# Two-layer graph attention on one core: transposes of float32 tiles moved from TensorE to 16-bit transposing transfers

## The chip, the cores and the metric

The kernel runs on one core of a Trainium2 chip. The time is device microseconds (us) of one execution; three executions of the kernel before took 3692.24, 3693.07 and 3693.68 us, the median is 3693.07. The engines of the core work side by side, each through its own list of instructions in order: TensorE (PE in the profile; PEld is its loading of weights), VectorE (DVE), ScalarE (ACT), GpSimd (POOL) and SyncE (SP, here the engine that starts most transfers).

## What is computed

There are 32 graphs of 512 nodes with 512 features each (`x`), and an adjacency matrix of 512x512 for each. Two attention layers follow each other, and each adds its result to `x`. Cut to what matters:

```python
h = maximum(layernorm(x), 0)
x = x + gat0(h, adj)                    # softmax over neighbours, one head of 512 features
h = maximum(layernorm(x), 0)
def gat_layer(x, mask, W, a_src, a_dst, bias, concat):
    xl = (x @ W).reshape(B, N, H, F)
    e = leaky_relu(asrc[:, :, None, :] + adst[:, None, :, :], 0.2)     # masked, then softmax over sources
    out = einsum('bsdh,bshf->bdhf', attn, xl)
    return (out.reshape(B, N, H * F) if concat else out.mean(axis=2)) + bias
g = elu(gat_layer(h, mask, W1, ..., b1, concat=True))                  # 4 heads of 256 features
x = x + gat_layer(g, mask, W2, ..., b2, concat=False)                  # 1 head of 512 features
```

Both products with weights, `h @ W1` and `g @ W2`, need their left operand with the features on the partitions, while `h` and `g` come out of the work before them with the nodes on the partitions. Between the two stands a transpose, and this is what the change moves.

## The kernel before

All values are float32; the masks are bf16. A graph's nodes are four tiles of 128 (`T = 4`). For each graph `b` the main loop emits, in this order: the masks, the product with W1 (`layer1_project`), the end of the graph before it (`load_back` of its `x` and `layer2_out`), the load of the graph after next, four times the edge weights and aggregate of a head (`layer1_scores`, `layer1_head`), then for graph `b + 1` the aggregate of layer 0 (`layer0_out`) and the input of layer 1 (`layer1_in`), for graph `b + 2` the scores of layer 0, and last the product with W2 (`layer2_project`).

That order isn't the one in which the instructions run. Each `op(...)` only records an engine or a choice of engines, a cost in nanoseconds, and what it reads and writes. The class `Plan` then makes several drafts of the whole program (a list scheduler: each engine takes the most urgent instruction that is ready by the costs), ranks the instructions anew after each by how late they may come, keeps the shortest draft and emits the instructions in its order. Once emitted, each engine's order is fixed: an instruction that waits holds up everything behind it on its engine. `on_pe`, `on_dve`, `on_act`, `on_pool` and `by_dma` give the costs. Buffers come from `slots`, a few places of each kind (three for edge weights `E`, six banks `acc` of TensorE's output, two for `x`); an instruction that opens a buffer is held back until a place is free.

The products with weights (`products`, L822) compute each 2x2 block product with seven partial products in place of eight; they need sums S1 to S4 of quarters of the left operand, which VectorE or GpSimd form (L803, L804), S1 being the sum of the two quarters of the later half of the nodes. The sums lie in places of `E`. A product of one graph is 56 matmuls for each layer. The aggregates (L627) are 64 matmuls for the four heads and 32 for each of layer 0 and layer 2.

The places that the change touches are these. In `layer1_in` four Relus (L510) write the normed tiles into a buffer of kind `h`; 16 TensorE transposes (`pe_transpose`, L487) turn them over into four banks, and ACT or DVE (`evict`, L520 and L526) copies each bank to `hT`. GpSimd then adds the bias `b2` to `x` (L750), and SP sends `x` to DRAM (L758, `spill`); it is brought back one graph later (L766). In `layer1_head` each tile's aggregate is scaled and given its bias (L893) into `v`. The bias was raised by 1 beforehand, so `v` holds z + 1, and elu(z) + 1 = max(z + 1, min(exp z, 1)) takes one Exp on ACT (L902) and one instruction on DVE (L905) for two tiles together. Eight transposes turn a head's result over, and the eviction takes the 1 off again:

```python
for k in range(nk):
    pt = Buffer("acc")
    for t in range(T):
        pe_transpose(0, pt, ..., v(t) + h1T("place"), ..., ident, t)
    evict(pt(*ROW), h1T(...), ..., N, bias=minus_one)
```

Other transposes on TensorE stay as they are: the columns spread into rows (`spread`, bank `m_bank`) and `in_lines` (L553). Transposing transfers of 16-bit values are in use already, for the masks (`transposed_mask`, L669), started by SP.

Of the kernel before, what the change touches and what calls it, by code (L numbers as in the profile page):

```python
# [10 lines left out]
BF16 = mybir.dt.bfloat16  # L11
AF = mybir.ActivationFunctionType
# [30 lines left out]
class Plan:  # L43
# [5 lines left out]
    DRAFTS = 6  # L49
# [61 lines left out]
    def latest(self, draft):  # L111
# [13 lines left out]
        for i in reversed(draft.order):  # L125
            occupied, there = self.cost(draft, i)[0], sum(self.cost(draft, i)[1:])
            for j in then[i]:
                late[i] = min(late[i], late[j] - (occupied if draft.engine[i] == "PE" == draft.engine[j] else there + self.SIGNAL))
        return late

    def draft(self, rank):
# [8 lines left out]
        lock, moving, landed = {"DVE": 0.0, "POOL": 0.0}, 0.0, []  # L140
# [23 lines left out]
        while len(draft.order) < len(ops):  # L164
# [19 lines left out]
            for buf in new:  # L184
                first = min(vacant[buf.kind], default=None)
# [24 lines left out]
            for held in moves:  # L210
                if len(landed) >= self.IN_FLIGHT:
                    at = max(at, landed[-self.IN_FLIGHT])
                moving = max(moving, at) + held
                there += moving - at
                landed.append(at + there)
# [39 lines left out]
def by_dma(n, after=2000.0):  # L255

    return 350.0, after, n / 300.0


@with_exitstack  # L260
def kernel(
# [51 lines left out]
    def places(kind, n, shape, dtype=F32, pool=big):  # L313
# [15 lines left out]
        "v": places("v", 2, [P, T, F]),  # L329
        "e": places("e", 1, [P, T // 2, F]),  # L330
        "col": places("col", 12, [P, T]),
        "ac": places("ac", 5, [P, 4, T]),
        "a_row": places("a_row", 1, [P, N]),
        "c_row": places("c_row", 1, [P, N]),
# [11 lines left out]
    plan = Plan(slots, ("x", "spill", "m0", "m0T", "m1", "m1T", "h", "hT", "pair", "xl2", "E", "E_one", "v", "a_row", "c_row", "a_bank"))  # L346
# [9 lines left out]
    minus_one = const.tile([P, 1], F32, name="minus_one")  # L356
    nc.vector.memset(minus_one, -1.0)
# [16 lines left out]
    b2_r = const.tile([P, D], F32, name="b2_r")  # L374
# [13 lines left out]
    def load_constants():  # L388
# [18 lines left out]
        fetch(HF, lambda: b1_r, rows(b1, HF), W["b1"](1), -LATER)  # L407
        fetch(D, lambda: b2_r, rows(b2, D), W["b2"](0), -LATER)
# [4 lines left out]
        for i in range(2):  # L413
# [5 lines left out]

        op(  # L420
            "DVE", on_dve(HF), lambda: nc.vector.tensor_scalar(b1_r, b1_r, 1.0, None, op0=ALU.add), W["b1"](1), W["b1"](0),
            -LATER,
        )
# [83 lines left out]
    def relu_normed(h, X, t, rstd, nmr):  # L507
# [3 lines left out]
                h.at[:, t, :D], X.at[:, t, :], AF.Relu, bias=nmr.at[:, t : t + 1], scale=rstd.at[:, t : t + 1]  # L511
            ),
            X((t, 0), (t, 1)) + rstd(0) + nmr(0), h(t),
        )

    def evict(src, dst, src_of, dst_of, n, bias=None, psum_half=False):

        def by_act():
            if bias is None:
                nc.scalar.copy(dst_of(), src_of())  # L520
            else:
                nc.scalar.activation(dst_of(), src_of(), AF.Identity, bias=bias)  # L522

        def by_dve():
            if bias is None:
                nc.vector.tensor_copy(dst_of(), src_of())  # L526
            else:
                nc.vector.tensor_scalar(dst_of(), src_of(), -1.0, None, op0=ALU.add)

        op(("ACT", "DVE"), (on_act(n, bias is not None), on_dve(n)), (by_act, by_dve), src, dst)  # L530
# [16 lines left out]
    def in_lines(ac, part, n):  # L547

        pt, flat_, lines = Buffer("acc"), Buffer("e"), Buffer("lines")
# [6 lines left out]
        evict(pt(0), flat_(0), lambda: pt.at[:m, :P], lambda: flat_.at[:m, 0, :P], P)  # L556
        op(
            "SP", by_dma(4 * m * P, 3000.0),
            lambda: nc.sync.dma_start(lines.at[:n].rearrange("n (t p) -> (n t) p", p=P), flat_.at[:m, 0, :P]),
# [4 lines left out]
    def row_of(kind, lines, k):  # L564

        row = Buffer(kind)
# [466 lines left out]
```

## Time and profile before

| what | value |
|---|---|
| median of three executions | 3693.07 us |
| the profiled execution | 3694.24 us |
| its span, first to last instruction | 3692.5 us |
| mean granted TensorE clock | 0.996 |
| one graph, once the loop is running | 112.6 us |
| busy in the span: PE, DVE, ACT, POOL | 3625.2, 2878.2, 1760.2, 1592.1 us |
| transfers: SP's queue, GpSimd's queue | 26.2%, 6.5% of 16 DMA engines' span |

Durations of single instructions come from the profiled execution. Starts of consecutive instructions on one engine lie closer than their durations say, as an instruction begins before the one ahead of it has ended; where a sum over many is wanted, the distance between starts is the measure. "Idle before, releaser" in a group's row is the time that the engine stood still just before those instructions, and what ended most of it.

### The profile page before, as it was taken

To read this page: it belongs to the slowest core of one execution; us is meant where nothing else is said; L and a number is where in the kernel's file an instruction comes from. 1 tells how busy PE (TensorE), PEld (TensorE's weight loads), DVE (VectorE), ACT (ScalarE), POOL (GpSimd) and SP (SyncE) were. 2 spreads that over 40 slices of the span, in tenths; PEclk is the share of its full clock that TensorE was granted. 3 is DMA by queue.
4 is the path that set the end of the run, shared out by engine and by line. 5 is a ranking of instruction groups with operands and counts; after the bars stand their busy time and mean duration, and the time that the engine had idled before them with its cause. 6 is when DMAs were issued, how large, how long until landed. Compare 5 with 4: busy or idle time off the path is not lost.

```text
span 3692.5 us, 51317 instructions
## 1 busy us (share of the span) xinstructions
PE 3625.2 (98%) x17806; PEld 3131.3 (85%) x17806; DVE 2878.2 (78%) x7478; ACT 1760.2 (48%) x3227; POOL 1592.1 (43%) x1353
## 2 busy tenths in 40 slices
PE   5899999999999999999999999999999999999998
PEld 4788888888888888888888888888888888888887
DVE  7988778877788877788877878777887778787755
ACT  2455444554454554445544445544455544455433
POOL 3534444534444444445344444444444444444332
PEclk9999999999999999999999999999999999999999
DMA  6244322334323333223333233442233422334310
GB/s 162 52 92 103 87 73 82 81 92 104 72 74 90 75 103 91 70 83 80 91 103 72 76 88 75 103 98 68 81 82 85 103 72 78 86 75 103 90 51 32
DMA packets 304342, 312.17 MB, mean 85 GB/s; under 512 B 150496, under 2 KB 188880, under 8 KB 304080
## 3 DMA queue, kind: packets, MB, share of 16 engines
q1 hardware_dynamic: 270288, 275.32, 26.2%
q0 software_dynamic: 33792, 33.56, 6.5%
q8 instruction: 140, 2.29, 0.3%
q14 instruction: 122, 1.00, 0.1%
HBM read 240.91 MB, written 67.89 MB: 84 GB/s over the span
## 4 chain that ended last, share of the span: by engine, by line
PE 94%; DVE 3%; DMA 1%; POOL 0%; issue 0%; ACT 0%; DVEq 0%; ACTq 0%
PE acc L627 46%; PE acc L822 41%; PE acc L487 4%; PE m_bank L487 2%; DVE junk L591 1%; DVE junk L378 0%; PE acc L553 0%; DVE E L612 0%; DMA m<-in_adj_dram 0%; DVE v L905 0%; POOL E_one L614 0%; DVE E_one L612 0%; DMA x<-in_x_dram 0%; DVE v L893 0%; DMA out_dram<-x 0%
## 5 line engine op out<-in xcount | busy, mean ns | idle before, releaser
L614 POOL TENSOR_TENSOR E<-E,m 128x512 f32<-128x512 f32 x512 | 620.2, 1240 | 803.3 <-DVE E L612 798.3
L627 PE MATMUL acc<-pair,E 128*128 128x257 f32 x4096 | 961.6, 381 | 1.4 <-ACT E L617 1.2
L627 PEld LDWEIGHTS acc<-pair,E 128*128 128x128 f32 x4096 | 743.0, 190 | 114.5 <-ACT E L617 14.4
L822 PE MATMUL acc<-w_T,E 128*128 128x257 f32 (+1 forms) x2048 | 521.5, 381 | 1.0 <-ACT pair L522 0.6
L627 PE MATMUL acc<-h,E_one 128*128 128x256 f32 (+1 forms) x2048 | 478.2, 382 | 6.3 <-ACT E_one L617 6.3
L617 ACT ACTIVATE E<-E 128x512 f32<-128x512 f32 x512 | 312.0, 624 | 315.4 <-POOL E L614 315.4
L627 PE MATMUL acc<-xl,E_one 128*128 128x257 f32 x1984 | 448.2, 379 | 0.0
L591 DVE CUSTOM_DVE_ANT_0 junk<-m1T,a_bank 128x512 bf16<-128x512 bf16 x640 | 436.0, 681 | 15.4 <-PE a_bank L487 1.7
L627 PEld LDWEIGHTS acc<-h,E_one 128*128 128x128 f32 x2048 | 383.8, 191 | 59.4 <-ACT E_one L617 7.6
L822 PEld LDWEIGHTS acc<-w_T,E 128*128 128x128 f32 x2048 | 379.6, 190 | 55.4 <-ACT pair L522 0.8
L627 PEld LDWEIGHTS acc<-xl,E_one 128*128 128x128 f32 x1984 | 371.4, 190 | 53.7
L612 DVE TENSOR_TENSOR E<-E,m_bank 128x512 f32<-128x512 f32 x512 | 326.5, 679 | 24.7 <-PE m_bank L487 24.7
L609 ACT ACTIVATE E<-c_row,ac 128x512 f32<-128x512 f32 x512 | 335.6, 708 | 1.9 <-DMA c_row<-lines 1.9
L520 ACT COPY pair<-acc 128x258 f32<-128x258 f32 (+1 forms) x375 | 138.2, 369 | 412.1 <-PE acc L822 410.3
L520 ACT COPY xl<-acc 128x257 f32<-128x257 f32 x219 | 81.7, 373 | 455.8 <-PE acc L822 455.8
L902 ACT ACTIVATE e<-v,minus_one 128x512 f32<-128x512 f32 x256 | 184.3, 720 | 236.4 <-DVE r L639 111.1
L645 DVE SCALAR_TENSOR_TENSOR x<-acc,r,x 128x256 f32<-128x256 f32 x512 | 240.6, 478 | 47.8 <-PE acc L627 43.6
L663 POOL DMA_DIRECT2D m<-in_adj_dram x64 | 51.4, 804 | 521.1 <-DVE col L591 476.8
L835 DVE TENSOR_TENSOR pair<-acc,pair 128x258 f32<-128x258 f32 (+1 forms) x390 | 164.5, 424 | 137.8 <-PE acc L822 127.7
L822 PE MATMUL acc<-w,hT 128*128 128x258 f32 x1024 | 268.4, 382 | 0.0
L822 PE MATMUL acc<-w,pair 128*128 128x257 f32 x1024 | 259.3, 380 | 0.0
L614 POOL TENSOR_TENSOR E_one<-E_one,m 128x512 f32<-128x512 f32 x128 | 145.0, 1165 | 263.2 <-DVE E_one L612 263.2
(108 smaller groups left out, 6117.7 us busy)
## 6 DMA issues: line engine op xcount, KB each, us to landing
a_row<-lines SPq DMA_DIRECT2D x190, 256.0 KB, 3.4
c_row<-lines SPq DMA_DIRECT2D x190, 256.0 KB, 3.5
x<-in_x_dram SPq DMA_DIRECT2D x32, 1024.0 KB
m<-in_adj_dram POOLq DMA_DIRECT2D x64, 512.0 KB, 7.0
spill<-x SPq DMA_DIRECT2D x32, 1024.0 KB, 4.3
x<-spill SPq DMA_DIRECT2D x32, 1024.0 KB
out_dram<-x SPq DMA_DIRECT2D x30, 1024.0 KB, 5.0
m0T<-m SPq DMA_TRANSPOSE x128, 4.2
```

Source lines behind the costliest of these rows:

```text
L487: op("PE", on_pe(P, transpose=True), lambda: nc.tensor.transpose(dst_of(), src_of(), identity), src, dst(part), ahead)
L520: nc.scalar.copy(dst_of(), src_of())
L591: lambda t=t: nc.vector.tensor_tensor_reduce(junk, mask_max.at[:, t, :], a_row.at, 1.0, LOWEST, ALU.add, ALU.max, accum_out=amax.at[:, t : ...
L609: lambda t=t: nc.scalar.activation(E.at[:, t, :], c_row.at, AF.Prelu, bias=a_of(t), scale=1.0, alpha=SLOPE),
L612: op("DVE", on_dve(N), lambda t=t: nc.vector.tensor_sub(E.at[:, t, :], E.at[:, t, :], m_row.at), m_row(*ROW) + E(t), E(t))
L614: "POOL", on_pool(N, True), lambda t=t: nc.gpsimd.tensor_add(E.at[:, t, :], E.at[:, t, :], mask.at[:, t, :]),
L617: op("ACT", on_act(N), lambda t=t: nc.scalar.activation(E.at[:, t, :], E.at[:, t, :], AF.Exp), E(t), E(t))
L627: lambda s=s: nc.tensor.matmul(acc.at[:, :n], E.at[:, s, node_block(t)], of(s), start=(s == 0), stop=(s == T - 1)),
L645: lambda acc=acc, r=r, f=f, t=t: nc.vector.scalar_tensor_tensor(X.at[:, t, f], acc.at[:, :HD], r.at, X.at[:, t, f], op0=ALU.mult, op1=ALU. ...
L822: lambda k=k: nc.tensor.matmul(acc.at[:, :width], at[a]()[:, k, node_block(r)], weight_of(w, k, c), start=(first and k == 0), stop=(k == n ...
L835: op("DVE", on_dve(width), lambda: nc.vector.tensor_add(place(), acc.at[:, :width], place()), acc(0) + token, token)
L902: op("ACT", on_act(2 * F, 1), lambda e=e, ts=ts: nc.scalar.activation(e.at, v.at[:, ts, :], AF.Exp, bias=minus_one), parts, e(0))
```

## The change

A float32 tile is turned over as two 16-bit halves. `turned` does it in three steps: ACT copies the tile of 128x512 float32, seen as 128x1024 values of 16 bits, into a second buffer so that all lower halves come first and all upper halves after them; SP starts one transposing transfer back into the first buffer, eight blocks of 128x128; ACT copies the result to its place, `hT` or `h1T`, and pairs lower and upper halves again. `layer1_in` calls it once for each node tile, `layer1_head` once for each pair of tiles of a head, so 12 times a graph.

Since such a copy can't subtract 1, the elu is now computed as max(z, -relu(1 - exp z)): Exp and a Relu on ACT, one instruction on DVE; `b1` is no longer raised. The normed tiles of layer 1 no longer take the place of kind `h`. The kinds `e`, `a_row` and `c_row`, one place each, become one kind `row` with four places, which the normed tiles, the second buffers of the turns, the elu's Exps, the rows of scores and the lines all share; `v` has four places of two tiles each, `col` and `ac` have fewer. The bias `b2` is added in DRAM: after `x` is spilled, GpSimd starts a transfer that adds `b2` to each of the 512 rows of the spilled copy. In the planner the costs of transposing transfers are new (`by_turning`, for the masks' too), transposing and other transfers are counted as two resources, and it makes 16 drafts in place of 6.

The core of the diff:

```diff
-    DRAFTS = 6
+    DRAFTS = 16
...
-                moving = max(moving, at) + held
-                there += moving - at
+                for k, held in enumerate(moves):
+                    taken[k] = max(taken[k], at) + held
+                there += max(taken[: len(moves)]) - at
...
+def by_turning(n):
+
+    return 1100.0 + n / 1000.0, 600.0, n / 300.0, 1400.0 + n / 180.0
...
-        "v": places("v", 2, [P, T, F]),
-        "e": places("e", 1, [P, T // 2, F]),
-        "col": places("col", 12, [P, T]),
-        "ac": places("ac", 5, [P, 4, T]),
-        "a_row": places("a_row", 1, [P, N]),
-        "c_row": places("c_row", 1, [P, N]),
+        "v": places("v", 4, [P, 2 * F]),
+        "row": places("row", 4, [P, N]),
+        "col": places("col", 10, [P, T]),
+        "ac": places("ac", 4, [P, 4, T]),
...
-    def relu_normed(h, X, t, rstd, nmr):
+    def relu_normed(place, token, X, t, rstd, nmr, also=()):
         op(
             "ACT", on_act(D, 2),
             lambda: nc.scalar.activation(
-                h.at[:, t, :D], X.at[:, t, :], AF.Relu, bias=nmr.at[:, t : t + 1], scale=rstd.at[:, t : t + 1]
+                place(), X.at[:, t, :], AF.Relu, bias=nmr.at[:, t : t + 1], scale=rstd.at[:, t : t + 1]
             ),
-            X((t, 0), (t, 1)) + rstd(0) + nmr(0), h(t),
-        )
-
...
+    def turned(values_of, src, e, place, results_of, dst):
+
+        def copied(out_of, in_of, reads, writes):
+            op(
+                "ACT", on_act(2 * N), lambda: nc.scalar.copy(out_of(), in_of()), reads, writes,
+            )
+
+        copied(
+            lambda: e.at.bitcast(U16).rearrange("p (b f) -> p b f", b=2),
+            lambda: values_of().bitcast(U16).rearrange("p (f b) -> p b f", b=2), src + place, e(0),
+        )
+        op(
+            "SP", by_turning(4 * P * N),
+            lambda: nc.sync.dma_start(
+                values_of().bitcast(U16).rearrange("p (c n) -> p c n", n=P), e.at.bitcast(U16), transpose=True
+            ),
+            e(0), src,
+        )
+
+        def paired():
+            out = results_of()
+            k, t = out.shape[1], out.shape[2]
+            return (
+                out.bitcast(U16).rearrange("p k t (n b) -> p k t n b", b=2),
+                values_of().bitcast(U16).rearrange("p (b t k n) -> p k t n b", b=2, k=k, t=t),
+            )
+
+        copied(lambda: paired()[0], lambda: paired()[1], src, dst)
...
-            relu_normed(hn, xb, t, rstd, nmr)
-        for k in range(KD):
-            pt = Buffer("acc")
-            for t in range(T):
-                pe_transpose(
-                    AHEAD, pt, lambda t=t, pt=pt: pt.at[:, node_block(t)], hn(t) + hT("place"),
-                    lambda t=t, k=k: hn.at[:, t, node_block(k)], ident, t,
-                )
-            evict(pt(*ROW), hT((k, 0), (k, 1)), lambda pt=pt: pt.at, lambda k=k: hT.at[:, k, :], N)
+            hn, e = Buffer("row"), Buffer("row")
+            relu_normed(lambda hn=hn: hn.at, hn(0), xb, t, rstd, nmr, e("place"))
+            turned(
+                lambda hn=hn: hn.at, hn(0), e, hT("place"),
+                lambda t=t: hT.at[:, :, node_block(t)].rearrange("p k (t n) -> p k t n", t=1), hT(*((k, t) for k in range(KD))),
+            )
...
         HT[b] = hT
-        for t in range(T):
-            op(
-                "POOL", on_pool(D), lambda t=t: nc.gpsimd.tensor_add(xb.at[:, t, :], xb.at[:, t, :], b2_r),
-                xb((t, 0), (t, 1)) + W["b2"](0), xb((t, 0), (t, 1)), lock=True,
-            )
-
 
         X.pop(b)
         S[b] = away = Buffer("spill")
         op(
             "SP", by_dma(4 * N * D), lambda: nc.sync.dma_start(away.at.rearrange("(t p) f -> p t f", p=P), xb.at),
             xb(*((t, half) for t in range(T) for half in range(2))), away(0),
+        )
+        op(
+            "POOL", (2200.0, 8000.0),
+            lambda: nc.gpsimd.dma_start(
+                away.at, bass.AP(tensor=b2.tensor, offset=b2.offset, ap=[[0, N], [1, D]]), accum_op=ALU.add
+            ),
+            away(0), away(0),
         )
 
...
-        v = Buffer("v")
-        for t in range(T):
-            acc = aggregate(E, t, xl, lambda s: ((j, s),), lambda s: xl_of(xl)[:, s, j, 2:], F + 1, v)
-            r = Buffer("r")
-            op("DVE", on_dve(8), lambda acc=acc, r=r: nc.vector.reciprocal(r.at, acc.at[:, F : F + 1]), acc(0) + xl(2), r(0))
-            op(
-                "DVE", on_dve(F, 1.0, True),
-                lambda t=t, acc=acc, r=r: nc.vector.scalar_tensor_tensor(
-                    v.at[:, t, :], acc.at[:, :F], r.at, b1_r[:, h * F : (h + 1) * F], op0=ALU.mult, op1=ALU.add
-                ),
-                acc(0) + r(0) + W["b1"](0), v(t),
-            )
-        for half in range(2):
-            ts = slice(half * T // 2, (half + 1) * T // 2)
-            parts = v(*range(T)[ts])
-            e = Buffer("e")
-            op("ACT", on_act(2 * F, 1), lambda e=e, ts=ts: nc.scalar.activation(e.at, v.at[:, ts, :], AF.Exp, bias=minus_one), parts, e(0))
-            op(
-                "DVE", on_dve(2 * F),
-                lambda e=e, ts=ts: nc.vector.scalar_tensor_tensor(
-                    v.at[:, ts, :], e.at, 1.0, v.at[:, ts, :], op0=ALU.min, op1=ALU.max
-                ),
-                parts + e(0), parts, lock=True,
-            )
         if j == 0:
             H1T.setdefault(b, []).append(Buffer("pair"))
         h1T = H1T[b][h // 2]
         nk = F // P
-        for k in range(nk):
-            pt = Buffer("acc")
-            for t in range(T):
-                pe_transpose(
-                    0, pt, lambda t=t, pt=pt: pt.at[:, node_block(t)], v(t) + h1T("place"), lambda t=t, k=k: v.at[:, t, node_block(k)], ident, t
+        for half in range(2):
+            ts = range(T)[half * T // 2 : (half + 1) * T // 2]
+            v, e = Buffer("v"), Buffer("row")
+            for i, t in enumerate(ts):
+                acc = aggregate(E, t, xl, lambda s: ((j, s),), lambda s: xl_of(xl)[:, s, j, 2:], F + 1, v)
+                r = Buffer("r")
+                op("DVE", on_dve(8), lambda acc=acc, r=r: nc.vector.reciprocal(r.at, acc.at[:, F : F + 1]), acc(0) + xl(2), r(0))
+                op(
+                    "DVE", on_dve(F, 1.0, True),
+                    lambda i=i, acc=acc, r=r, v=v: nc.vector.scalar_tensor_tensor(
+                        v.at[:, i * F : (i + 1) * F], acc.at[:, :F], r.at, b1_r[:, h * F : (h + 1) * F],
+                        op0=ALU.mult, op1=ALU.add,
+                    ),
+                    acc(0) + r(0) + W["b1"](0), v(i),
                 )
-            evict(pt(*ROW), h1T((j * nk + k, 0), (j * nk + k, 1)), lambda pt=pt: pt.at, lambda k=k: h1T_of(h1T)[:, j * nk + k, :], N, bias=minus_one)
+            op("ACT", on_act(2 * F), lambda e=e, v=v: nc.scalar.activation(e.at, v.at, AF.Exp), v(0, 1), e(0))
+            op(
+                "ACT", on_act(2 * F, 1),
+                lambda e=e: nc.scalar.activation(e.at, e.at, AF.Relu, bias=one, scale=-1.0), e(0), e(0),
+            )
+            op(
+                "DVE", on_dve(2 * F),
+                lambda e=e, v=v: nc.vector.scalar_tensor_tensor(v.at, e.at, -1.0, v.at, op0=ALU.mult, op1=ALU.max),
+                v(0, 1) + e(0), v(0, 1), lock=True,
+            )
+            turned(
+                lambda v=v: v.at, v(0, 1), Buffer("row"), h1T("place"),
+                lambda half=half: h1T_of(h1T)[:, j * nk : (j + 1) * nk, half * HN : (half + 1) * HN].rearrange(
+                    "p k (t n) -> p k t n", n=P
+                ),
+                h1T(*((j * nk + k, half) for k in range(nk))),
+            )
 
```

## The prediction

> **What bounds the kernel now.** I read the page from the top: the busy shares, then the chain that ended last, then the groups of instructions, then one period of the timeline. From the page, the busy time of each engine (busy us, share, instructions) and the chain by engine and by line:
>
> ```profile
> PE 3625.2 (98%) x17806; PEld 3131.3 (85%) x17806; DVE 2878.2 (78%) x7478; ACT 1760.2 (48%) x3227; POOL 1592.1 (43%) x1353
> ...
> PE 94%; DVE 3%; DMA 1%; POOL 0%; issue 0%; ACT 0%; DVEq 0%; ACTq 0%
> ```
>
> The reader is to see that TensorE is busy 98% and carries 94% of the chain: what leaves TensorE leaves the time, as long as nothing new makes it wait. The chain shows the same piece of layer 2's product (52 matmuls, L822) again and again at one distance:
>
> ```profile
> 1521.11 11.30 PE acc L822 x52
> 1633.73 11.30 PE acc L822 x52
> ```
>
> So one graph takes 112.6 us. Within that period (1408.5 to 1521.1 us) the engines were busy 112.60 (PE), 88.54 (DVE), 54.58 (ACT) and 49.39 us (POOL): TensorE has no gap at all. The groups to be removed, and two operations I use as prices (columns: line, engine, operation, operands, shapes, count, then busy us, mean ns, idle time before them):
>
> ```profile
> L487 PE MATMUL acc<-ident,v 128*128 128x128 f32 x1024 | 164.4, 273 | 2.4 <-DVE v L905 2.4
> L522 ACT ACTIVATE pair<-acc,minus_one 128x512 f32<-128x512 f32 x133 | 90.5, 682 | 111.8 <-PE acc L487 111.7
> L487 PE MATMUL acc<-ident,h 128*128 128x128 f32 x512 | 78.4, 278 | 7.0 <-ACT h L510 7.0
> L750 POOL TENSOR_TENSOR x<-x,b_r 128x512 f32<-128x512 f32 x128 | 162.2, 1298 | 34.6 <-ACT h L510 34.6
> ```
>
> Mean durations overlap on TensorE, so the price is the distance between starts. From the timeline of TensorE (start us, length us):
>
> ```profile
> 1476.62 0.60 PE L487 MATMUL acc<-ident,v 128*128 128x128 f32 x4
> 1477.06 2.33 PE L627 MATMUL acc<-pair,E 128*128 128x257 f32 x10
> ```
>
> Four transposes advance the engine by 0.44 us: 0.109 each. One matmul record of 128x257 advances it 0.217 us and a float32 matmul is two of them: 0.4345 us. What a 16-bit turning transfer costs, from the timeline of SP's queue and the issues (the last number is median us from issue to landing):
>
> ```profile
> 1442.73 2.51 SPq L669 DMA_TRANSPOSE m1T<-m  x2
> ...
> m0T<-m SPq DMA_TRANSPOSE x128, 4.2
> m1T<-m SPq DMA_TRANSPOSE x128, 2.4
> ```
>
> For 128x512 values of 16 bits SP is held 1.2 us; looked at in slices of 0.1 us, the data move only after that, for 0.7 us at some 215 GB/s, and it lands 0.5 us later: 2.4 in all. m0T's, which share the queues with a mask load, take 4.2.
>
> **What the Trainium skill says.** "DMA: Bandwidth & Descriptors", section "DMA Transpose (X-bar)": transposing transfers take 2-byte types only, write SBUF, and come from SP's or ACT's queue; hence the split of float32 into halves, and SP. The trace has them on SP with bf16. "VectorE: DVE Perf Modes", section "The three transpose paths", puts a 128x128 block at 390 ns on TensorE and 1309 on the transfer: TensorE's is 0.109 here when streamed, so the measurement decides; four blocks in 2.4 us fit. "SBUF — State Buffer", section "Door 1: The DMA port swizzle", says that accesses that leave a 16-byte line each time pay a penalty; the second copy alternates between halves 1 KB apart. No run here shows that pattern.
>
> **The change, part by part.** The planner's order of the changed kernel has 8590 TensorE instructions instead of 10126: 1536 transposes fewer (512 of normed inputs, 1024 of heads' results), 48 a graph. 1536 x 0.109 = 167 us off TensorE. Nothing takes their place there.
>
> ACT: 384 turns with two copies of 128x1024 16-bit values each. Price: the skill's "ScalarE: Activation LUTs", section "What ACT_TABLE_LOAD costs", has 0.833 ns an element and 93 ns between back-to-back instructions, 0.95 us (estimate); the trace's float32 Exp advances 0.53 us for 512, which agrees. 768 x 0.95 = 730 us; 256 new Relus of 0.62 (the pace of four L609 in 2.55 us) 159; evictions removed: 133 x 0.6 + 70 x 0.5 = -115. ACT goes from 1760 to about 2530 us, 71% of 3570. The first copy is safe; the second I take at 0.95 too, at most 1.9 if each access pays.
>
> DVE loses 123 + 58 evictions of 0.69 (-125 us). POOL loses L750, -162 us, for 32 accumulating transfers. Those wait on POOL for the spill to land (4.3 us), and mostly a memset and the next sums stand behind them; the sum is needed a whole graph later, when x comes back. POOL is idle over half the period, so I cost this at nothing, and 1 to 3 us a graph if its 1 MB of additions slows the turns beside it; that is not shown before.
>
> SP: 12 turns a graph of 256 KB. The issue lies between 1.36 us (the planner's figure) and 2.4 (twice 1.2); data 1.25 us at the measured rate; 0.5 to land: 3.2 to 4.2, I take 3.7 from issue to landing. SP's sum is 12 x 2 + 8 x 1.2 + about 25 x 0.4 = 44 of 107 us. Data for all: 384 x 256 KB at 215 GB/s, 470 us of a 3570 us span.
>
> What matters is whether two chains are covered. **Heads' end:** after the last aggregate, reciprocal and L893 0.64, Exp, Relu and maximum 0.7 + 0.7 + 0.7, copy 1.0, hand-overs 0.5: 4.2; turn 3.7; copy 1.0; first sum of layer 2 (POOL, L804) 1.3: 10.2 us. In the new order TensorE has 28 matmuls there (18 of layer 0's, 10 of layer 2's), 12.2 us. Covered by 2 us. The final copy stands on ACT behind two h activations that wait for layer 0's last matmuls, no later than that. **Layer 1's input:** norm 3.5, two Relus and a copy to 5.9, turn to 9.6, copy back, Relu and copy of tile 2 to 12.2 (four row buffers allow two tiles at once), turn to 15.9, then tile 3's Relu, copy back and copy to 18.5; on SP its turn is behind x coming back and two row loads, 1.5 MB at about 300 GB/s, so it lands near 23.7; copy 1.0, two sums 2.3: 27. With the accumulate beside it, 28. TensorE's cover is all 56 matmuls of layer 2's product and 16 of layer 1's: 31.5 us. Covered by 3 to 4.
>
> In between, ACT's second copies wait in order. In the new order the work on ACT between the two copies of a head's turn is 3.75 us on average by these prices, about the turn; the shorter gaps miss 1.5 us (turn 3.4) to 5.8 (turn 4.4) a graph, and ACT in the heads' stretch has 35.7 us of work against 46.1 of TensorE's. So waits are mostly absorbed; queued behind them are Exps of E and evictions of acc, for which TensorE waits if late. I allow 1 us a period, 31 in all (0 to 3 a period). The start: the first graph has nothing to lay over layer 1's input chain (TensorE waits there already), +10; the last graph's heads' end has a half of layer 2's aggregates over it and a chain 4 us longer than now, +5.
>
> Sum: span 3692.5 - 167 + 31 + 10 + 5 = 3571.5. The profiled execution took 3694.24, 1.7 more than its span and 1.2 more than the median of 3693.07; so 3572 as a median.
>
> **Rivals.** (1) Everything hides: 3525 + 15 and no stalls, 3540; DVE (44.2 busy of 46.5 us in the heads' stretch now, 2.6 of it removed) speaks a little against it. (2) The second copy runs at half rate: 8 x 0.95 = 7.6 us more in the heads' stretch, 43.3 of 46.1, and with waits of 2 to 5 us TensorE stalls some 3 us a graph more: 3571 + 31 x 3, about 3660. (3) Slower, by one mechanism: the turns take longer than planned, and ACT's in-order waits on them replace the transposes. If load costs them what it costs m0T (4.2 - 2.4 = 1.8), a turn is 5.5: the input chain becomes 28 + 3 x 1.8 = 33.4, 1.9 late; heads wait 8 x (5.6 - 3.75) = 14.8 on ACT with 10.4 spare, 4.4 late; 6.3 lost against 5.2 gained: 3693 + 31 x 1.1 + 15, about 3742. It decides from a turn of about 5.3 us on. For it: m0T's 4.2, and that order and buffers leave little to spare. Against it: in the heads' stretch the transfers are idle now (21% busy). (4) That the change doesn't do what it says is excluded by the counts.
>
> **Chances.** The likeliest case with rival 1: 0.46, its own range 3530 to 3640. Rival 2: 0.11. Within 0.2% (7 us, about what can be told from no change): 0.04. Rival 3 and worse: 0.39, of which 0.14 lies over 3850. Faster 0.57, same 0.04, slower 0.39. For 8 in 10 the range goes from 3530, where nothing stalls, to 3850.
>
> **What would show it.** Right: TensorE's transposes gone, period 107 to 109 us, ACT's copies near 1.0 us, turns landing in 3.2 to 4.2, TensorE's idle before L822 and L627 matmuls small. Wrong: ACT's longest waits on the turning transfers and TensorE idle behind late Exps or evictions; copies near 2 us; or the period ending on the sums of layer 1 whose last tile comes late. The forecast fails if turns land after 5 us or the two covers are shorter than counted.

## The result, and the profile after

The changed kernel takes 3986.54 us (median of four executions, 3979.25 to 3990.85), the kernel before beside it 3692.65: a ratio of 1.079, 95% interval 1.0775 to 1.0812. The forecast was 3572 us, with a range of 3530 to 3850. The transposes did go, and yet one graph takes 120.1 us in place of 112.6 (from start to start of the spills, five graphs on from 549.73 us; later graphs take somewhat longer: from there on it is 121.5 on average over 26 graphs).

From the page after: busy time by engine, the chain by engine and by line, then groups (columns as before) and issues of transfers.

```profile
PE 3571.2 (90%) x16270; PEld 3024.4 (76%) x16270; DVE 2775.1 (70%) x7356; ACT 2532.6 (63%) x4039; POOL 1385.6 (35%) x1206
...
PE 25%; DVE 24%; DMA 22%; ACT 20%; issue 4%; POOL 3%; SPq 1%; DVEq 0%; ACTq 0%; POOLq 0%
DMA row<-row 16%; PE acc L842 14%; PE acc L649 11%; DVE junk L613 6%; ACT row L529 4%; DVE E L634 3%; ACT row L928 3%; ACT pair L529 2%; ACT E L639 2%; DMA m<-in_adj_dram 2%; DVE x L667 2%; ACT row L925 2%; DMA row<-lines 2%; ACT hT L529 2%; ACT row L509 2%
...
L529 ACT COPY hT<-row 128x1024 uint16<-128x1024 uint16 x128 | 147.7, 1154 | 470.7 <-DMA row<-row 470.7
...
L842 PE MATMUL acc<-w_T,pair 128*128 128x257 f32 x512 | 165.4, 475 | 193.2 <-ACT xl L519 160.1
...
L529 ACT COPY pair<-v 128x1024 uint16<-128x1024 uint16 x256 | 295.1, 1153 | 20.9 <-DMA v<-row 17.8
...
L529 ACT COPY row<-v 128x1024 uint16<-128x1024 uint16 x256 | 263.3, 1038 | 28.9 <-DVE v L932 28.3
...
spill<-in_L_gnn_b_dram POOLq DMA_DIRECT2D x32, 1024.0 KB, 14.8
...
v<-row SPq DMA_TRANSPOSE x256, 3.0
```

TensorE's share of the chain fell from 94% to 25%, and the largest single entry is now a transfer, `row<-row`: the turns of layer 1's input. ACT stood 470.7 us before the copies that wait for those turns, but only 20.9 before the copies of the heads' turns, though these are twice as many. The heads' turns land in 3.0 us (the median; the profile has the landing of 29 of the 256). So turning is not slow in itself; something stands beside the input's turns. The transfer that adds `b2` takes 14.8 us from issue to landing. TensorE's largest wait follows from ACT's: 160.1 us before matmuls of layer 2's product, until ACT's eviction `xl<-acc` of earlier results of that product frees a bank.

One graph shows it. From the timeline after, engine by engine (start us, length us; in brackets the idle time before and its releaser):

```profile
1885.73 1.13 POOL L776 DMA_DIRECT2D spill<-in_L_gnn_b_dram  x1
...
1889.91 11.04 SPq L538 DMA_TRANSPOSE row<-row  x2
...
1902.04 1.16 ACT L529 COPY hT<-row 128x1024 uint16<-128x1024 uint16 x1 [10.94 <-DMA row<-row]
...
1903.26 0.36 ACT L519 COPY xl<-acc 128x257 f32<-128x257 f32 x1
...
1899.25 1.90 PE L842 MATMUL acc<-w_T,pair 128*128 128x257 f32 x8
1905.43 2.09 PE L842 MATMUL acc<-w,hT 128*128 128x258 f32 x4 [4.28 <-ACT hT L529]
...
1921.83 5.44 PE L842 MATMUL acc<-w_T,E 128*128 128x258 f32 x16 [4.14 <-POOL E L824]
```

GpSimd starts the adding transfer 4 us before the first turns. SP, whose issue of a turn otherwise takes 1.23 us (the median of the heads' turns), is held for 11 us by two of them. ACT waits 10.94 us for the first; queued behind that copy is the eviction `xl<-acc`, and TensorE, which needs the bank or the turned tile, stops for 4.28 us. Later the sums of layer 1 come late too, and it stops for 4.14. What the transfer engines carried between 1890 and 1895 us (queue, packets, MB, share of the 16 engines; q0 is GpSimd's queue, q1 is SP's):

```profile
q0 software_dynamic: 297, 0.60, 104.4%
q1 hardware_dynamic: 48, 0.01, 1.1%
```

The two turns are issued, but hardly a packet of theirs moves while the additions fill the engines; in the next 5 us GpSimd's queue takes 26.9% and SP's 109.8%. The stretches around it (length; busy us and instructions of PE, PEld, DVE, ACT, POOL; granted clock, share of the transfer engines, GB/s):

```profile
1895.00:1900.00 5.00, 5.00 (x25) 4.36 (x24) 0.85 (x2) 0.00 (x0) 0.00 (x0) 1.00 1.38 56
1900.00:1905.00 5.00, 1.15 (x6) 0.66 (x4) 0.43 (x1) 2.96 (x5) 0.00 (x0) 1.00 0.49 80
1905.00:1910.00 5.00, 4.57 (x14) 3.77 (x15) 0.13 (x1) 1.70 (x3) 0.00 (x0) 0.66 0.69 157
```

Between 1895 and 1900 the transfer engines are full (a share above 1 is packets lying over each other) and move only 56 GB/s. And after the idle time the granted clock is 0.66: part of the stall is paid a second time.

### The profile page after: what moved, and what is told of

It reads as the page before. It is cut to its first block, busy times and chain, and to the rows that moved or that the text cites. A ratio compares the mean times of both kernels' runs of the same rounds, so it can differ in the third digit from the quotient of the medians.

```text
span 3989.1 us, 49533 instructions
## 1 busy us (share of the span) xinstructions
PE 3571.2 (90%) x16270; PEld 3024.4 (76%) x16270; DVE 2775.1 (70%) x7356; ACT 2532.6 (63%) x4039; POOL 1385.6 (35%) x1206
## 4 chain that ended last, share of the span: by engine, by line
PE 25%; DVE 24%; DMA 22%; ACT 20%; issue 4%; POOL 3%; SPq 1%; DVEq 0%; ACTq 0%; POOLq 0%
DMA row<-row 16%; PE acc L842 14%; PE acc L649 11%; DVE junk L613 6%; ACT row L529 4%; DVE E L634 3%; ACT row L928 3%; ACT pair L529 2%; ACT E L639 2%; DMA m<-in_adj_dram 2%; DVE x L667 2%; ACT row L925 2%; DMA row<-lines 2%; ACT hT L529 2%; ACT row L509 2%
## 5 line engine op out<-in xcount | busy, mean ns | idle before, releaser
L649 PE MATMUL acc<-pair,E 128*128 128x257 f32 x4096 | 943.3, 382 | 25.2 <-ACT E L639 24.6
L649 PEld LDWEIGHTS acc<-pair,E 128*128 128x128 f32 x4096 | 763.1, 190 | 157.4 <-ACT E L639 51.5
L613 DVE CUSTOM_DVE_ANT_0 junk<-m1T,a_bank 128x512 bf16<-128x512 bf16 x640 | 436.4, 682 | 37.1 <-DMA row<-lines 12.1
L529 ACT COPY hT<-row 128x1024 uint16<-128x1024 uint16 x128 | 147.7, 1154 | 470.7 <-DMA row<-row 470.7
L649 PEld LDWEIGHTS acc<-h,E_one 128*128 128x128 f32 x2048 | 387.6, 190 | 69.5 <-ACT E_one L639 11.4
L519 ACT COPY pair<-acc 128x258 f32<-128x258 f32 (+1 forms) x445 | 164.7, 371 | 327.0 <-PE acc L842 325.1
L631 ACT ACTIVATE E<-row,ac 128x512 f32<-128x512 f32 x512 | 338.1, 708 | 6.0 <-DMA row<-lines 5.1
L842 PE MATMUL acc<-w_T,pair 128*128 128x257 f32 x512 | 165.4, 475 | 193.2 <-ACT xl L519 160.1
L529 ACT COPY pair<-v 128x1024 uint16<-128x1024 uint16 x256 | 295.1, 1153 | 20.9 <-DMA v<-row 17.8
L842 PEld LDWEIGHTS acc<-w_T,pair 128*128 128x128 f32 x512 | 119.2, 239 | 225.3 <-ACT xl L519 167.8
L529 ACT COPY row<-v 128x1024 uint16<-128x1024 uint16 x256 | 263.3, 1038 | 28.9 <-DVE v L932 28.3
L842 PEld LDWEIGHTS acc<-w,hT 128*128 128x128 f32 x1024 | 203.8, 203 | 86.8 <-ACT hT L529 35.8
## 6 DMA issues: line engine op xcount, KB each, us to landing
spill<-in_L_gnn_b_dram POOLq DMA_DIRECT2D x32, 1024.0 KB, 14.8
```

What stands on the lines that cost most here:

```text
L519: (lambda: nc.scalar.copy(dst_of(), src_of()), lambda: nc.vector.tensor_copy(dst_of(), src_of())), src, dst,
L529: "ACT", on_act(2 * N), lambda: nc.scalar.copy(out_of(), in_of()), reads, writes,
L613: lambda t=t: nc.vector.tensor_tensor_reduce(junk, mask_max.at[:, t, :], a_row.at, 1.0, LOWEST, ALU.add, ALU.max, accum_out=amax.at[:, t : ...
L631: lambda t=t: nc.scalar.activation(E.at[:, t, :], c_row.at, AF.Prelu, bias=a_of(t), scale=1.0, alpha=SLOPE),
L649: lambda s=s: nc.tensor.matmul(acc.at[:, :n], E.at[:, s, node_block(t)], of(s), start=(s == 0), stop=(s == T - 1)),
L842: lambda k=k: nc.tensor.matmul(acc.at[:, :width], at[a]()[:, k, node_block(r)], weight_of(w, k, c), start=(first and k == 0), stop=(k == n ...
```

## The experiments

### What the adding transfer costs

**Without it.** The planner still counts it, so the order on every engine stays; only the instruction is left out.

```diff
-            lambda: nc.gpsimd.dma_start(
-                away.at, bass.AP(tensor=b2.tensor, offset=b2.offset, ap=[[0, N], [1, D]]), accum_op=ALU.add
-            ),
+            lambda: None,
```

> The changed kernel without the adding transfer; the planner still counts it, so every engine keeps its order. b2 is left out of the result. Theory A (the adding transfer, 14.8 us from issue to landing, holds SP's queue and the turns of layer 1's input behind it): most of the 470.7 us that ACT waits for those turns goes, 3560 to 3660 us. Rival B (the chain of layer 1's input is too long even with free queues, since the turns follow each other over four row buffers): still over 3850. Rival C (ACT's in-order second copies and their 1.15 us in place of 0.95 cost the heads' stretch): over 3750, with TensorE idle behind the heads.

Measured: 3653.12 us (3649.33 to 3656.34), ratio 0.989 [0.9879, 0.9908]. The transfer costs 3986.5 - 3653.1 = 333 us, 10.4 a graph. Of the two profiled spans' difference, 334.6 us, TensorE's idle time makes 266 (417.9 against 151.8); the other 68.5 is busy time (3571.2 against 3502.7) for the same instructions in the same order, at a mean clock of 0.961 against 0.991.

**A plain copy in its place.** The same 1 MB by the same queue, read from the one row of `b2`, written elsewhere in DRAM.

```diff
-                away.at, bass.AP(tensor=b2.tensor, offset=b2.offset, ap=[[0, N], [1, D]]), accum_op=ALU.add
+                spare, bass.AP(tensor=b2.tensor, offset=b2.offset, ap=[[0, N], [1, D]])
```

> In the place of the adding transfer a plain one of the same size, from the same queue and with the same source, into a spare DRAM buffer; b2 is left out of the result. Theory A in the form that it is the adding (reading and writing back) that takes 14.8 us: the plain one lands in 5 to 8 us and the time is within 60 us of the run without any. In the form that any megabyte on GpSimd's queue holds the turns: 3850 to 3990, as with the adding.

Measured: 3890.94 us, within the range expected if any megabyte on GpSimd's queue holds the turns, though it lands sooner than the adding one. 238 of the 333 us are there without any adding.

**Another source.** `b2` is written into 512 rows of DRAM once, and the adding transfer reads those.

```diff
+    wide = spill.tile([N, D + 16], F32, tag="wide", name="wide")
+    nc.gpsimd.dma_start(wide[:, :D], bass.AP(tensor=b2.tensor, offset=b2.offset, ap=[[0, N], [1, D]]))
...
-                away.at, bass.AP(tensor=b2.tensor, offset=b2.offset, ap=[[0, N], [1, D]]), accum_op=ALU.add
+                away.at, wide[:, :D], accum_op=ALU.add
```

> The changed kernel, with b2 written once into 512 rows of DRAM and the adding transfer reading those instead of the one row again and again. If reading one row 512 times makes the transfer slow, it falls from 14.8 us to some 5 (a plain spill of 1 MB is 4.5) and most of the 333 us come back, to 3660 to 3720. If the adding in DRAM itself is slow, it stays at 13 to 15 us and the time above 3900.

Measured: 3844.68 us, between the two expectations. Then the same source and no adding:

```diff
-                away.at, wide[:, :D], accum_op=ALU.add
+                spare, wide[:, :D]
```

> As the kernel whose adding transfer reads 512 written-out rows (3845 us), but the transfer only copies those rows to another place in DRAM and adds nothing; b2 is left out. If both the repeated row and the adding cost, it lands in some 5 us instead of 10.0 and the time is 3690 to 3740. If moving 1 MB from DRAM to DRAM on this queue costs 10 us whatever it does, it stays near 10 and the time near 3840.

Measured: 3750.24 us, 10 above the range expected if both the repeated row and the adding cost. The issues of the transfer on the three pages (median us from issue to landing last), the plain copy of one row first:

```profile
spare<-in_L_gnn_b_dram POOLq DMA_DIRECT2D x32, 1024.0 KB, 10.7
```

adding from 512 rows:

```profile
spill<-wide POOLq DMA_DIRECT2D x32, 1024.0 KB, 10.0
```

and the plain copy of 512 rows:

```profile
spare<-wide POOLq DMA_DIRECT2D x32, 1024.0 KB, 6.3
```

| 1 MB by GpSimd's queue | issue to landing, us | ACT's wait for input turns, us | time, us | over no transfer |
|---|---|---|---|---|
| none | - | 107.1 | 3653 | 0 |
| copy, 512 rows | 6.3 | 225.4 | 3750 | +97 |
| add, 512 rows | 10.0 | 318.4 | 3845 | +192 |
| copy, one row read 512 times | 10.7 | 383.7 | 3891 | +238 |
| add, one row read 512 times | 14.8 | 470.7 | 3987 | +333 |

The three parts add up: moving 1 MB there at all costs 97 us, reading one row again and again 141 (in both pairs: 238 - 97, 333 - 192), adding 95 (192 - 97, 333 - 238). Over the range, each microsecond of landing costs (3987 - 3750) / (14.8 - 6.3) = 28 us, 0.87 a graph. Two limits: the middle three rows are one execution each, and four executions of the changed kernel lie 11.6 us apart; and the plain copies don't have to wait for the spill to land, so "adding" includes that wait (in the changed kernel GpSimd waits 4.5 us for it in all).

**In four pieces** of 128 rows, planned and issued one by one.

```diff
-            "POOL", (2200.0, 8000.0),
...
-            away(0), away(0),
+        for t in range(T):
+            op(
+                "POOL", (1200.0, 3700.0),
...
+                    away.at[node_block(t)], bass.AP(tensor=b2.tensor, offset=b2.offset, ap=[[0, P], [1, D]]), accum_op=ALU.add
...
+                away(t), away(t),
```

> The adding transfer of the changed kernel in four pieces of 128 rows, planned and issued one by one. If a turn waits because a whole 1 MB of additions stands ahead of it on the same DMA engines, a piece takes 14.8 / 4 = 3.7 us, no turn waits longer than some 6 us unless pieces stand back to back, and a good part of the 333 us comes back: 3750 to 3880. If the pieces are issued back to back it stays at 3950 to 4000. If the fixed part of each transfer is what costs, each piece still takes 10 us or more and the time goes above 4050.

Measured: 3874.27 us (3871.12 to 3876.42), ratio 1.049 [1.0473, 1.0508]. From its timeline of GpSimd and of SP:

```profile
1945.12 3.47 POOL L777 DMA_DIRECT2D spill<-in_L_gnn_b_dram  x4
...
1947.87 18.91 SPq L538 DMA_TRANSPOSE row<-row  x3
```

The pieces were issued back to back, for which 3950 to 4000 was expected; 112 us came back nevertheless, and the time is at the upper end of the first range. ACT's wait for the input's turns fell from 470.7 to 356.2 us, yet its longest is 14.1. Each piece lands in 9.0 us (median), so the expected 3.7 is refuted too. The planner drew up another order for the pieces, so how much of the 112 us is the size of a block and how much is the order isn't settled.

**After the turns.** The planner is told that the adding transfer reads the turned tiles, so that it puts it behind the turns in its order; nothing on the chip waits for that.

```diff
-            away(0), away(0),
+            away(0) + hT(*((k, t) for k in range(KD) for t in range(T))), away(0),
```

> The changed kernel with the adding transfer held back until the four turns of layer 1's input have been copied to hT. Theory A: the turns land in 3 to 4 us again and most of the loss goes; the transfer then stands beside the masks' transposing transfers and the rows, which have more to spare: 3680 to 3760. If any transfer of that kind beside any transposing one costs as much: over 3880.

Measured: 3932.63 us (3930.05 to 3933.94), ratio 1.065 [1.0633, 1.0665]. Two graphs from its timelines of GpSimd and ACT, one with the transfer after the turns, one with it beside the last two:

```profile
1170.09 1.13 POOL L776 DMA_DIRECT2D spill<-in_L_gnn_b_dram  x1
1275.77 1.15 POOL L776 DMA_DIRECT2D spill<-in_L_gnn_b_dram  x1 [0.43 <-issue]
...
1187.56 0.59 ACT L601 COPY a_bank<-row 128x512 f32<-128x512 f32 x1 [6.46 <-DMA row<-lines]
...
1291.70 1.16 ACT L529 COPY hT<-row 128x1024 uint16<-128x1024 uint16 x1 [10.92 <-DMA row<-row]
```

With the transfer moved away from the turns, ACT waits 6.46 us for the rows of scores (over the span 200.3 us, against 68.4 in the changed kernel); where the order slips, the transfer stands beside turns again and ACT waits 10.92 us for one. The time is in the range of the second expectation, but in the loop about every second graph is of the second kind and doesn't test what was meant, and the order is a new one. So this run only says that the place tried isn't free.

**In the kernel before.** Only `b2` is moved to DRAM, with the adding transfer of the changed kernel; all transposes stay on TensorE, the planner is the old one.

```diff
-        for t in range(T):
-            op(
-                "POOL", on_pool(D), lambda t=t: nc.gpsimd.tensor_add(xb.at[:, t, :], xb.at[:, t, :], b2_r),
...
+                away.at, bass.AP(tensor=b2.tensor, offset=b2.offset, ap=[[0, N], [1, D]]), accum_op=ALU.add
```

> The kernel before with only the addition of b2 moved into DRAM; transposes stay on TensorE. Theory A: the adding transfer costs only where turns stand behind it, so 3670 to 3710 us, no difference that matters. If adding in DRAM is itself costly (queues held for x coming back and for the rows), over 3750.

Measured: 3735.33 us (3732.05 to 3737.7), ratio 1.012 [1.0101, 1.0131], between the two expectations. The same transfer, landing in 15.7 us here, costs 43 us where only the masks' turns and row loads are near it, and 333 where every input tile passes through a turn. (GpSimd's 162 us of additions are gone in both, and the 43 us hold a new draft of the order as well.)

### What the turns bring without it

**b2 by GpSimd again**, before the spill as in the kernel before, everything else as changed (`v` has three places, as the row of `b2` takes room again).

```diff
-        "v": places("v", 4, [P, 2 * F]),
+        "v": places("v", 3, [P, 2 * F]),
...
+                "POOL", on_pool(D), lambda t=t: nc.gpsimd.tensor_add(xb.at[:, t, :], xb.at[:, t, :], b2_r),
```

> The changed kernel with b2 added by GpSimd in SBUF as before, planned anew; three places of v in place of four make room for the row of b2. Theory A: 3560 to 3660 us, faster than the kernel before. Rivals B and C: over 3750.

Measured: 3739.26 us (3736.46 to 3740.8), ratio 1.0125 [1.0108, 1.0142]. It lies between the two expectations. From its waits (us in total, times, longest):

```profile
POOL x L771 <- ACT row L511: 192.0, 87, 7.0
...
PE m_bank L488 <- DVE col L622: 53.3, 52, 4.1
PE acc L842 <- DVE pair L855: 40.0, 24, 3.9
```

GpSimd's additions must follow the Relus, which now come tile by tile with the turns, so they wait 192 us in order (34.6 before), and TensorE waits more on columns and on results that VectorE adds up (30.4 and 16.9 in the run without `b2`). Taking `b2` back into SBUF costs 3739 - 3653 = 86 us against leaving it out; three places of `v` and another order are part of that. With the additions after `x` has come back instead:

```diff
-        for t in range(T):
-            op(
-                "POOL", on_pool(D), lambda t=t: nc.gpsimd.tensor_add(xb.at[:, t, :], xb.at[:, t, :], b2_r),
...
             away(0), xb(*((t, half) for t in range(T) for half in range(2))),
         )
+        for t in range(T):
+            op(
+                "POOL", on_pool(D), lambda t=t: nc.gpsimd.tensor_add(xb.at[:, t, :], xb.at[:, t, :], b2_r),
```

> Both turned by transfers, b2 added by GpSimd in SBUF after x comes back from DRAM instead of before it leaves; three places of v. If the 86 us between the run with b2 on GpSimd and the run without any b2 come from GpSimd's additions waiting behind the late Relus of layer 1's input (192 us of waits there): 3640 to 3670 us. If they come from three places of v: still 3710 to 3750.

Measured: 3689.88 us (3683.18 to 3693.69), ratio 0.999 [0.9984, 0.9997], within 0.2% of the kernel before. It lies between the two expectations: 49 of the 86 us came back. GpSimd waits longer here than before, 339.1 us for `x` to come back, so the length of its wait alone doesn't set the price, and how the other 37 us divide between the places of `v`, the additions and the order isn't separated.

**The planner alone** in the kernel before:

```diff
-    DRAFTS = 6
+    DRAFTS = 16
...
-                "SP", (2200.0, 3000.0, 600.0),
+                "SP", by_turning(2 * P * N),
```

> The kernel before with only the planner of the changed one (16 drafts, new costs for the masks' transfers, two resources). If the planner by itself matters, over 3710 or under 3675 us; I expect 3685 to 3700, and with that the rest of the difference belongs to the turns and the addition of b2.

Measured: 3716.25 us (3714.66 to 3716.99), ratio 1.006 [1.0048, 1.0078]: 24 us lost, more than expected, so the planner matters by itself.

**Only the heads turned**: layer 1's input goes through TensorE, GpSimd adds `b2` before the spill, `v` has three places, the planner is the new one.

```diff
-            hn, e = Buffer("row"), Buffer("row")
-            relu_normed(lambda hn=hn: hn.at, hn(0), xb, t, rstd, nmr, e("place"))
-            turned(
...
+                pe_transpose(
+                    AHEAD, pt, lambda t=t, pt=pt: pt.at[:, node_block(t)], hn(t) + hT("place"),
```

> Only the heads' results turned by transfers; layer 1's input by TensorE and b2 by GpSimd in SBUF as before; three places of v. Theory D (the heads' turns are covered, as each landed in 3.0 us; what is left of the loss without the adding transfer comes from layer 1's input): 3693 - 1024 x 0.109 + 15, 3580 to 3620 us. Rival C (ACT's in-order copies cost the heads' stretch): 3660 or more.

Measured: 3654.40 us (3653.99 to 3654.76), ratio 0.990 [0.9881, 0.9911], between the two expectations. Of the kernels that leave no part out it is the fastest: 1.0% faster than the kernel before, 8.3% than the changed one. And with the planner of before (the heads' turns, which it didn't know, are priced in its form: 1240 ns of issue, 2400 ns after it, and 300 bytes a ns):

```diff
-    DRAFTS = 16
+    DRAFTS = 6
...
-                "SP", by_turning(2 * P * N),
+                "SP", (2200.0, 3000.0, 600.0),
```

> Only the heads' results are turned by transfers, layer 1's input stays with TensorE and b2 with GpSimd, as in the kernel with the heads alone (3654 us), but with the planner of before: its 6 drafts, its old costs of transfers, one resource for all of them. The planner alone cost 24 us when put into the kernel before. If that loss adds up, this comes to 3654 - 24 = 3630 (3615 to 3640). If the new costs of turning are needed for the order around the turns, it comes to 3654 or above.

Measured: 3710.37 us (3708.38 to 3713.18), ratio 1.005 [1.0033, 1.0066]. The expected 3630 is refuted: with turns in the program the new planner saves 56 us, without them it costs 24. Its price can't be taken from one kernel to the other.

**Only the input turned**, the heads on TensorE:

```diff
-        for k in range(KD):
-            pt = Buffer("acc")
...
+            turned(
+                lambda hn=hn: hn.at, hn(0), e, hT("place"),
```

> The new planner, the heads turned by TensorE as before, and only layer 1's input by transfers, four turns a graph; b2 is left out of the sum, with nothing in its place. 512 transposes fewer are 512 x 0.109 = 56 us. If the chain of the input is covered as predicted: 3716 - 56 = 3660 (3650 to 3672). If it isn't, and this is where the rest of the gain went: 3690 or above.

Measured: 3795.49 us (3789.9 to 3802.45), ratio 1.028 [1.0265, 1.0296]: 79 us above the planner alone, where 56 below was forecast. From its chain (start us, length us), one graph:

```profile
1583.20 5.12 DMA row<-row
...
1592.56 11.58 PE acc L849 x52
...
1606.18 1.19 SPq L705
1607.41 1.26 SPq L705
1608.72 1.26 SPq L705
...
1611.60 8.03 DMA row<-lines
```

In this graph the product with `hT` runs on without a gap; what ends late are the rows of scores. Their loads stand on SP behind the issues of the masks' turns, and then take 8 us (7.2 in the median; 3.7 and 3.4 for the two rows under the planner alone). Over the whole span the loads of rows and the input's turns have 6% of the chain each, so one graph doesn't settle which of them costs more. The order that the planner drew up for this kernel is its own, so the 79 us belong to this order and not to the four turns alone.

## Why the prediction was wrong

**The step that failed** is the accumulate in "The change, part by part": "I cost this at nothing, and 1 to 3 us a graph if its 1 MB of additions slows the turns beside it". It slows them so much that the kernel loses 10.4 us a graph, 333 in all. That alone turns the sign: without the transfer the same order runs in 3653 us, 1.1% faster than before. In "Layer 1's input" the same term was one microsecond of a chain, "28" against a cover of 31.5; in the graph shown the first turn alone was issued at 1889.91 us and its copy started at 1902.04, 12.1 us later where 3.7 had been counted. The prediction asked on which engine the transfer waits (GpSimd, idle enough) and when its sum is needed (a graph later), both rightly. It did not ask what else passes through the transfer engines in those 15 us. The Trainium skill has the point: "DMA: Bandwidth & Descriptors", section "Issuing engines are not separate DMA queues", says that transfers started by different engines end on the same 16 and interleave. The runs agree (the additions took 104.4% of the engines while the turns issued beside them took 1.1%), and show its price here: a copy that nobody waits for costs 97 us. A turn goes from SBUF to SBUF and touches no DRAM; what it shares with the transfer are the engines that move both. The sign of being wrong that the prediction had named came true: ACT's longest waits for transfers are on the turns, and TensorE stands idle behind late evictions.

**Rival 3** had the sign and the consequence, late turns replacing transposes through ACT's in-order waits, but not the cause. It raised every turn to 5.5 us; the heads' turns land in 3.0. Its argument against itself, that the transfers are idle in the heads' stretch, held; the crowd stood in the input's stretch, brought there by the change itself.

**TensorE, ACT, the turn.** Right: 1536 transposes gone, ACT 2532.6 us busy (2530 forecast), turns not slower than priced where nothing stands beside them (the heads': issue 1.23 us, landing 3.0, both medians; 3.7 taken). The second copy takes 1.15 us against 1.04 for the first: alternating halves cost some 0.1 us, and rival 2 (1.9) is out. The prediction's remark that four blocks in 2.4 us fit 1309 ns a block doesn't come out (four would be 5.2); its sums use the measured 2.4, so nothing rests on it.

**Heads' end.** Covered, as predicted: ACT's wait for heads' turns is 17.8 us in the changed kernel, and without the adding transfer TensorE stands 4.1 us in all until such a turn has been copied back (`PE acc<-w,pair`, released by `ACT pair`). The heads alone, against the planner alone, gain 3716 - 3654 = 62 us, where 1024 transposes at 0.109 are 111. TensorE's busy time falls from 3632.2 to 3551.4 us there, 0.079 for each transpose in place of 0.109, the distance between starts. Idle time takes the other 19.

**Layer 1's input.** The removed 512 transposes brought nothing in any pair measured, though no pair differs by that alone: 3653 with the input turned and `b2` free against 3654 for the heads alone with `b2` added; 3690 with `b2` after the return; 79 lost with the input alone. The cover itself held: in the kernel without the transfer ACT still waits 107.1 us for these turns, 4.4 at most, but TensorE only 11.4 us in all for the sums of layer 1 (258 wide), 9.3 for those of GpSimd and 2.1 for those of VectorE:

```profile
L840 PE MATMUL acc<-w_T,E 128*128 128x258 f32 x1024 | 269.9, 391 | 27.6 <-DVE pair L853 14.9 <-POOL E L822 9.3 <-DVE E L821 2.1
```

Where the gain of these 512 went isn't shown.

**Stalls.** "I allow 1 us a period" was too little even without the transfer: its period is 111.0 us (from 620.64 to 1064.64 in four graphs), not 107 to 109. From the groups of TensorE without the transfer (idle us before, and the releaser, last):

```profile
L649 PE MATMUL acc<-pair,E 128*128 128x257 f32 x4096 | 944.1, 382 | 23.3 <-ACT E L639 23.0
L840 PE MATMUL acc<-w_T,E 128*128 128x257 f32 (+1 forms) x2048 | 523.8, 385 | 32.6 <-DVE pair L853 14.9 <-POOL E L822 11.2 <-DVE E L821 5.0
...
L486 PE MATMUL m_bank<-ident,col 128*128 128x128 f32 x768 | 119.4, 278 | 30.6 <-DVE col L620 30.4
```

The same three groups of the kernel before stood 1.4, 1.0 and 15.8 us: TensorE waits a little for everybody. That ACT has 775 us more to do in order is a likely reason, but isn't shown to be the one. The span is 83 us above the forecast's (3654.5 against 3571.5). TensorE's idle time is 151.8 us (its span less its busy time, 3654.5 - 3502.7) against 113 in the forecast's sum (67 before, 46 added): 39. The other 44 are busy time, 3502.7 against 3625.2 - 167. At the 0.079 that the heads alone gave, 1536 transposes are 121 us and not 167, and 3625.2 - 121 = 3504 comes out. Part of that may be the clock: the mean, 0.991 against 0.996, would make 18 of the 44. With the input alone the price doesn't hold (TensorE busy 3633.6 us, with 512 transposes fewer than the planner alone, at a clock of 0.990 against 0.997), so it stays an estimate.

## What to carry to other kernels

A transfer whose result nobody needs soon is not free: look at what else moves in the microseconds until it lands, and whether an engine that works in order waits for that. When work leaves the bounding engine for a shared resource, price the resource in the stretch where it lands, not over the span. Take the parts of a change apart before judging it: the heads' part alone was 1.0% faster, the whole 7.9% slower.

## What was not expected of the hardware

- A transfer of 1 MB from DRAM to DRAM on GpSimd's queue landed in 6.3 us from 512 rows and in 10.7 from one row read 512 times; adding made it 10.0 and 14.8. A plain spill of 1 MB from SBUF beside them landed in 4.5.
- The issue of a turning transfer is held too: 11.04 us for two, and 18.91 for three beside the four pieces, in place of 1.23 each, so that everything behind it on SP waits as well. A median doesn't show it: over the 128 turns of the input the issue takes 1.28 us in the median and 10.53 at most.
- After 4.28 us of idle time TensorE's clock was 0.66 in a slice of 5 us, and four matmul records took 2.09 us, not the 1.03 of other groups of four. The Trainium skill, "TensorE: Matmul & The Clock Gate", section "What's actually happening", says that the clock halves after about 3.4 us without work and returns after as long a busy time; the trace agrees: an estimate from that figure, 3.4 us at half and 1.6 at full in a slice of 5, is 0.66. The trace's clock record for that place is half clock from 1905.13 us on, for 3.41 us. Over the span there are 43 such stretches with 314.5 us in all, against 11 with 68.1 us without the adding transfer; the mean clock is 0.961 against 0.991. So a stall of that length costs more than the time that TensorE stands still.
